# Graph attention's f column goes through DRAM to all partitions, in a four-layer graph kernel ordered by a planner

## The chip, the cores and the metric

The kernel runs on one core of a Trainium2 chip. The metric is the device time of one execution in microseconds (us). The core's engines each work through their own queue of instructions in order: TensorE (PE in the profile, its weight loads PEld), VectorE (DVE), ScalarE (ACT), GpSimd (POOL) and SyncE (SP, which here issues the transfers). They wait for each other through semaphores.

## What is computed

There are 64 graphs of 256 nodes with 256 features each, and an integer adjacency matrix of 256 x 256 for each graph. Four layers follow each other, every one wrapped as `x = layernorm(x + layer(x, adj))`:

```
layer 0: transformer block: 8-head attention masked by adj | adj.T | eye, then a 256-1024-256 feed-forward
layer 1: graph attention (GAT) with bias
layer 2: graph attention, then elu
layer 3: two relational convolutions (root weight, relation adj == 1, divided by the degree), each with elu
```

The change is in the two graph-attention layers. Cut to what matters, one of them is

```
Wh = h @ W                                   # 256 nodes x 256
f, g = Wh @ a1, Wh @ a2                      # one number a node, twice
e = leaky_relu(f[:, None] + g[None, :], 0.2)
e = where(adj > 0, e, -1e9)
out = softmax(e, axis=-1) @ Wh
```

The kernel holds e transposed: the partition is the node that g belongs to, and along the free dimension run the nodes of f. So every partition needs the whole row of 256 f values.

## The kernel before

A graph is two blocks of 128 nodes (NB = 2), and all of a graph's work is float32 apart from masks. Nothing is written out engine by engine by hand. The function `graph(g)` describes one graph's operations one after the other: each has an engine, a planned duration in us (the first number of `pe(...)`, `dve(...)`, `act(...)`, `pool(...)`), the tiles it reads and writes, and for VectorE and GpSimd whether it is taken to use the port that the two share (`"uses"`, `"waits"`). All 64 graphs' operations go into one `Plan`. `Plan.schedule` (line 112) then plays them through as a list scheduler: an operation is ready when its predecessors are done, an engine that is free takes the ready operation with the earliest due time (counted back from `PERIOD`, 46 us a graph), provided that the rings have buffers for its tiles. The order that comes out is the order of issue on every engine. So planned durations do nothing on the chip by themselves; they decide the order, and through it which graph's work stands beside which.

Four details of the planner matter for the change. `LAG` is the time that passes between an operation's end and the moment at which another engine sees it (3.5 for SP, 0.08 to 0.21 for the others). `SWITCH` is added to a matrix operation whose mode (`full`, `row`, `col`: how the array is partitioned) differs from the one before it. A buffer ring ("h" has 3 buffers, "e" 4, "bank" the 8 PSUM banks) bounds how many such tiles are in flight. And the readiness of a follower is

```
seen = end + self.LAG[e]
a.ready = max(a.ready, end if a.engine == e else seen + self.TO.get(a.engine, 0.0))
```

so a follower on the same engine counts as ready at the end, without the lag.

Graph attention is `gat` (line 767). It transposes x (L596, copied to a tile T on L599), multiplies by W widened with the two columns a1 and a2 (L605; `gw`), which leaves Wh, f and g side by side in a PSUM bank, and copies that to the SBUF tile `h` (by VectorE on L778 in layer 1, by ScalarE on L776 in layer 2). `spread` (L785 to L790) then brings f to all partitions: for each block of nodes, the f column, repeated 128 times, is transposed by TensorE against the identity, so that a bank `pf` holds f along its free dimension in every partition. VectorE forms e from it, one instruction for each block (L792: add g, take the minimum with the mask `gm`) and one for the leaky relu (L795); ScalarE takes the exponential (L797); TensorE multiplies e by h (L605 again, "bank<-h,e"); L802 is the reciprocal of the row sum. On GpSimd, L781 squares f and g for a check of the value range, and L619 to L622 compute the reciprocal root of each layer norm, which ScalarE applies on L626.

SyncE's queue holds the loads (adj twice a graph, x, and x again as xr: L579) and the stores of the result (L902).

After the planned part, a few values collected on the way decide whether a general path, lines 930 on, computes everything again in a safer way. It is not taken with these inputs.

Of the kernel before, what the change touches and what calls it, by code (L numbers as in the profile page):

```python
# [17 lines left out]
P = 128  # L18
# [6 lines left out]
RINGS = {"x": 3, "adj": 4, "bits": 2, "am": 2, "gm": 6, "T": 5, "qk": 2, "v": 2, "p": 12, "both": 4, "inv": 1, "ctxT": 2, "X": 9,  # L25
         "xr": 2, "hid": 1, "h": 3, "e": 4, "n": 2, "rel": 3, "hi": 2, "lo": 2, "o": 4}
SMALL = {"mv": 8, "st": 4, "rstd": 8, "r": 6, "rdeg": 4}
# [23 lines left out]
class Plan:  # L51
# [7 lines left out]
    TO = {"PE": 0.06, "POOL": 0.05}  # L59
    SWITCH = 0.2  # L60
    PERIOD = 46.0
# [144 lines left out]
def tile_gnn_stack(ctx: ExitStack, tc: tile.TileContext, t: dict, out: bass.AP):  # L206
# [113 lines left out]
    nc.vector.tensor_copy(ident_b, ident)  # L320
    ones_b = filled([P, P], BF16, "ones_b", 1.0)
    ones = filled([P, HD], F32, "ones", 1.0)
    neghalf = filled([P, NT], F32, "neghalf", -0.5)
    eye = filled([P, N // P, N], BF16, "eye", 0.0)
    for h in range(N // P):
        nc.vector.tensor_copy(eye[:, h, h * P : (h + 1) * P], ident_b)
    gcol, bcol = cols("ln1_g", KB), cols("ln1_b", KB)
# [152 lines left out]
    def main_path(plan):  # L480
# [9 lines left out]
        for name, bufs in SMALL.items():  # L490
            ring(name, bufs)
        plan.ring("bank", 8, bank)

        c_wqkv, c_wo, c_w1, c_w2, c_b1, c_bo = (plan.fixed(w) for w in (wqkv, wo, w1, w2, b1, bo))
# [60 lines left out]
        def graph(g):  # L555
# [9 lines left out]
            def act(cost, issue, reads, writes):  # L565
                op("ACT", cost, issue, reads, writes)

            def pool(cost, issue, reads, writes, port="uses"):
                op("POOL", cost, issue, reads, writes, port=port)

            def new(ring, shape, dtype=F32):
                return plan.tile(ring, shape, dtype)
# [16 lines left out]
            def transposed(xt):  # L589

                xT, pt = new("T", [P, KB, N]), new("bank", [P, KB, N])

                def issue():
                    for kb in range(KB):
                        for i in range(NB):
                            nc.tensor.transpose(pt()[:, kb, i * P : (i + 1) * P], xt()[:, i, kb * P : (kb + 1) * P], ident)  # L596

                pe("full", 0.44, issue, [xt], [pt], [xT])
                act(0.48, lambda: nc.scalar.copy(xT(), pt()), [pt], [xT])  # L599
                return xT  # L600
# [6 lines left out]
            def layer_norm(y):  # L607

                mv, stat = new("mv", [P, NB, 2]), new("st", [P, NB, 6])
                rstd = new("rstd", [P, 2, NB])  # L610

                def stats():
                    for i in range(NB):
                        nc.vector.bn_stats(stat()[:, i, :], y()[:, i, :])  # L614
                    for i in range(NB):
                        nc.vector.bn_aggr(mv()[:, i, :], stat()[:, i, :])  # L616

                def root():
# [10 lines left out]
                dve(1.0, stats, [y], [mv, stat])  # L629
                pool(1.5, root, [mv], [rstd], port="waits")  # L630
                act(1.0, apply, [y, rstd], [y])
# [25 lines left out]
            def projections(xT):  # L657
# [22 lines left out]
                act(0.49, lambda: nc.scalar.copy(v(), pv()), [pv], [v])  # L680
                return qk, v

            def attention(xT, am):
# [6 lines left out]
                for kt in range(NB):  # L690
# [10 lines left out]

                    pe("row", 1.08, scores, [qk], s, [p[kt, r] for r in range(4)])
                    for r in range(4):
                        pr, k = p[kt, r], 8 * g + 4 * kt + r
                        act(0.61, lambda pr=pr, k=k, sr=s[r]: nc.scalar.activation(  # L705
                            pr(), sr(), AF.Exp, accum_out=seen_sum[:, k : k + 1]), [s[r]], [pr])
                        dve(0.60, lambda pr=pr, kt=kt: nc.vector.tensor_tensor(  # L707
                            pr(), pr(), am()[:, kt, None, :].to_broadcast([P, KB, N]), op=ALU.mult), [pr, am], [pr], "uses")
# [5 lines left out]
                for hg in range(KB):  # L714
                    pc = new("bank", [P, 2, N])

                    def values(hg=hg, pc=pc):
# [8 lines left out]

                    pe("col", 1.31, values, [v] + both + list(p.values()), [pc], [ctxT, inv])
                    dve(1.67, lambda hg=hg, pc=pc: nc.vector.reciprocal(inv()[:, hg, :], pc()[:, 1, :]), [pc], [(inv, hg)])  # L728
                    dve(0.34, lambda hg=hg, pc=pc: nc.vector.tensor_tensor(
                        ctxT()[:, hg, :], pc()[:, 0, :], inv()[:, hg, :], op=ALU.mult), [pc, (inv, hg)], [(ctxT, hg)])  # L730
                act(0.61, lambda: nc.scalar.activation(inv(), inv(), AF.Identity, accum_out=seen_inv[:, g : g + 1]), [inv], [inv])
                return ctxT

            def product_plus(lhs, reads, rhs, n, add):

                y, po = tok("X"), new("bank", [P, NB, D])
                for i in range(NB):
                    pe("full", 0.43 * n, lambda i=i: product(po()[:, i, :], lambda c: lhs(c)[:, i * P : (i + 1) * P], rhs, n),
                       reads, [po], [y])
                dve(0.66, lambda: nc.vector.tensor_tensor(y(), po(), add(), op=ALU.add), [po, add], [y])  # L740
                return y
# [25 lines left out]
            def gat(xt, layer, gm, seen, bias, finish):  # L767
# [3 lines left out]
                for i in range(NB):  # L771
# [3 lines left out]
                    if bias is None:  # L775
                        act(0.29, lambda i=i, ph=ph: nc.scalar.copy(h()[:, i, 0 : D + 2], ph()), [ph], [(h, i)])  # L776
                    else:
# [4 lines left out]
                                                          h()[:, :, F_COL : G_COL + 1], op=ALU.mult), [(h, 0), (h, 1)], [], "waits")  # L782
                pf = new("bank", [P, N])

                def spread():  # L785
                    for i in range(NB):
                        nc.tensor.transpose(pf()[:, i * P : (i + 1) * P],
                                            h()[:, i, F_COL : F_COL + 1].to_broadcast([P, P]), ident)

                pe("full", 0.22, spread, [(h, 0), (h, 1)], [pf], [e])  # L790
                for i in range(NB):
                    dve(0.40, lambda i=i: nc.vector.scalar_tensor_tensor(e()[:, i, :], pf(), h()[:, i, G_COL : G_COL + 1],  # L792
                                                                         gm()[:, i, :], op0=ALU.add, op1=ALU.min),
                        [pf, (h, i), gm], [(e, i)])
                dve(0.60, lambda: nc.vector.scalar_tensor_tensor(e(), e(), SLOPE, e(), op0=ALU.mult, op1=ALU.max), [e], [e],  # L795
                    "uses")
                act(0.52, lambda: nc.scalar.activation(e(), e(), AF.Exp), [e], [e])  # L797
                for i in range(NB):
                    po, r = new("bank", [P, HW]), new("r", [P, 1])
                    pe("full", 0.87, lambda i=i, po=po: product(po(), lambda kt: e()[:, kt, i * P : (i + 1) * P],  # L800
                                                                lambda kt: h()[:, kt, :], NB), [e, h], [po], [z, r])
                    dve(0.12, lambda po=po, r=r: nc.vector.reciprocal(r(), po()[:, ONE : ONE + 1]), [po], [r])  # L802
                    finish(i, z, po, r)
# [12 lines left out]
            def layer2(xt, gm):  # L816
                def finish(i, z, po, r):
# [4 lines left out]
                                                                     op1=ALU.add), [po, r, xt], [(z, i)])  # L822
                    dve(0.37, lambda: nc.vector.scalar_tensor_tensor(n(), n(), 1.0, xt()[:, i, :], op0=ALU.min,
                                                                     op1=ALU.add), [n, xt], [n], "uses")
                    dve(0.37, lambda: nc.vector.scalar_tensor_tensor(zi(), n(), -1.0, zi(), op0=ALU.add, op1=ALU.max),
                        [n, (z, i)], [(z, i)], "uses")
# [15 lines left out]
            def conv(h, layer, rel, rdeg):  # L842
# [18 lines left out]
                for j in range(NB):  # L861
# [7 lines left out]

                    pe("full", 0.46, gather, [rel, hi, lo], [pa])  # L870
                    if layer == 0:
# [37 lines left out]

    with tc.tile_pool(name="work", bufs=1) as pools["work"], tc.manual_schedule():  # L910
        main_path(Plan())
# [181 lines left out]
    wrong = nc.values_load(bad_i, min_val=0, max_val=4 * P)  # L1093
    with tc.tile_pool(name="general", bufs=1) as pools["work"], tc.If(wrong > 0):
        w_rel0 = []
        for i in (1, 2):
# [62 lines left out]
```

## Time and profile before

| | us |
|---|---|
| median of 3 runs | 3038.87 |
| lowest, highest of the 3 | 3038.41, 3041.54 |
| the profiled execution | 3041.5 |
| its span, from the first to the last instruction | 3039.6 |
| VectorE busy | 2560.6 (84%) |
| ScalarE busy | 1574.8 (52%) |
| GpSimd busy | 761.8 (25%) |

The profiled execution is 1.9 us longer than its span, and its granted TensorE clock was 0.994. "Busy" counts from an instruction's start to its end, and neighbours overlap in an engine's pipeline, so a mean duration is longer than the time by which one instruction pushes back the next. For that the profile's chain of work is of use: it cuts each stretch of time to the instruction that carried it.

### The profile page before, as it was taken

How to read it: one execution, taken by the hardware profiler on the slowest of the kernel's cores; microseconds unless marked ns; L12 is line 12 of the kernel's file. 1: busy time of each engine (PE TensorE's matmuls, PEld its weight loads, DVE VectorE, ACT ScalarE, POOL GpSimd, SP SyncE). 2: the span in 40 equal slices, each digit the busy share in tenths (PEclk: the TensorE clock that was granted, in tenths of full speed). 3: DMA queues.
4: the chain of work that ended last, by engine and by line, in shares of the span. 5: the costliest groups of instructions: out<-in, count | busy, mean ns of one | idle time of the engine just before them, and what ended most of it. 6: DMA issues, size and time to landing. Idle time of an engine off the chain costs nothing.

```text
span 3039.6 us, 49429 instructions
## 1 busy us (share of the span) xinstructions
PE 2949.0 (97%) x17462; PEld 2257.9 (74%) x17462; DVE 2560.6 (84%) x6368; ACT 1574.8 (52%) x3777; POOL 761.8 (25%) x1877
## 2 busy tenths in 40 slices
PE   8999999999999999999999999999999999999897
PEld 6777767777777777777777777777777777777584
DVE  6889798888797987988889888979889879897857
ACT  3455445555554554555455455545555545555444
POOL 2222222222222222222232222222222223222121
PEclk9999999999999999999999999999999999999999
DMA  5001011111010010010110101100101110001000
GB/s 155 25 22 36 19 34 32 29 28 32 22 32 29 29 36 28 25 32 28 29 32 25 36 22 32 32 29 28 30 27 29 29 31 29 28 25 29 8 11 15
DMA packets 91947, 93.56 MB, mean 31 GB/s; under 512 B 5648, under 2 KB 90896, under 8 KB 91696
## 3 DMA queue, kind: packets, MB, share of 16 engines
q1 hardware_dynamic: 91072, 89.15, 9.9%
q8 instruction: 141, 2.31, 0.3%
q0 software_dynamic: 624, 1.19, 0.2%
q14 instruction: 110, 0.90, 0.1%
HBM read 73.54 MB, written 16.78 MB: 30 GB/s over the span
## 4 chain that ended last, share of the span: by engine, by line
PE 71%; DVE 19%; ACT 4%; POOL 3%; issue 2%; SPq 1%; DMA 0%; POOLq 0%; ACTq 0%; DVEq 0%
PE bank L605 57%; PE bank L596 4%; PE bank L724 3%; PE bank L867 3%; DVE p L707 2%; PE bank L699 2%; PE bank L719 2%; DVE st L614 2%; ACT X L626 1%; POOL rstd L620 1%; ACT p L705 1%; DVE o L877 1%; DVE inv L728 1%; DVE both L711 1%; DVE X L740 1%
## 5 line engine op out<-in xcount | busy, mean ns | idle before, releaser
L619 POOL TENSOR_SCALAR rstd<-mv 128x2 f32<-128x2 f32 x384 | 134.0, 349 | 1535.2 <-DVE mv L616 1388.5
L605 PE MATMUL bank<-T,w 128*128 128x256 f32 x2048 | 480.7, 381 | 2.0 <-ACT T L599 1.4
L605 PE MATMUL bank<-cw,T 128*128 128x512 f32 x1024 | 469.7, 601 | 11.3 <-ACT T L599 8.8
L626 ACT ACTIVATE X<-X,rstd 128x256 f32<-128x256 f32 x640 | 349.8, 596 | 236.8 <-POOL rstd L622 151.2
L605 PE MATMUL bank<-w,hid 128*128 128x256 f32 x2048 | 463.3, 380 | 0.0
L605 PEld LDWEIGHTS bank<-w,hid 128*128 128x128 f32 x2048 | 383.5, 190 | 58.6 <-issue 5.1
L605 PEld LDWEIGHTS bank<-T,w 128*128 128x128 f32 x2048 | 376.6, 190 | 58.2 <-issue 5.1
L707 DVE TENSOR_TENSOR p<-p,am 128x512 f32<-128x512 f32 x512 | 329.0, 683 | 31.6 <-ACT p L705 30.2
L605 PEld LDWEIGHTS bank<-cw,T 128*128 128x128 f32 x1024 | 192.0, 192 | 212.6 <-issue 186.2
L705 ACT ACTIVATE p<-bank 128x512 f32<-128x512 f32 x512 | 300.7, 599 | 46.7 <-PE bank L699 45.9
L620 POOL TENSOR_TENSOR rstd<-rstd,neghalf 128x2 f32<-128x2 f32 x384 | 311.2, 810 | 32.0
L599 ACT COPY T<-bank 128x512 f32<-128x512 f32 x384 | 222.0, 586 | 184.8 <-PE bank L596 181.2
L605 PE MATMUL bank<-h,e 128*128 128x259 f32 x1024 | 251.3, 386 | 9.5 <-ACT e L797 7.1
L605 PE MATMUL bank<-T,wqkv 128*128 128x256 f32 x1024 | 247.4, 384 | 6.6 <-ACT T L599 6.6
L757 ACT ACTIVATE hid<-bank,col_b 128x256 f32<-128x256 f32 x512 | 212.1, 472 | 74.8 <-PE bank L605 72.7
L605 PE MATMUL bank<-gw,T 128*128 128x258 f32 x1024 | 247.1, 382 | 1.3 <-ACT T L599 1.2
L614 DVE BATCH_NORM_STATS2 st<-X 128x6 f32<-128x256 f32 x640 | 239.2, 416 | 5.1
L605 PEld LDWEIGHTS bank<-h,e 128*128 128x128 f32 x1024 | 190.7, 190 | 67.4 <-issue 28.0
L728 DVE RECIPROCAL inv<-bank 128x256 f32<-128x256 f32 x128 | 215.3, 1721 | 8.7 <-PE bank L724 8.7
L605 PEld LDWEIGHTS bank<-T,wqkv 128*128 128x128 f32 x1024 | 188.8, 191 | 37.4 <-ACT T L599 9.8
L605 PEld LDWEIGHTS bank<-gw,T 128*128 128x128 f32 x1024 | 190.0, 190 | 32.1 <-ACT T L599 3.2
L781 POOL TENSOR_TENSOR seen_fg<-h 128x4 f32<-128x4 f32 x128 | 54.8, 428 | 624.0 <-DVE h L778 322.7
(124 smaller groups left out, 4966.6 us busy)
## 6 DMA issues: line engine op xcount, KB each, us to landing
adj<-in_adj_dram SPq DMA_DIRECT2D x128, 256.0 KB, 2.8
x<-in_x_dram SPq DMA_DIRECT2D x64, 256.0 KB, 2.8
xr<-in_x_dram SPq DMA_DIRECT2D x64, 256.0 KB, 2.8
out_dram<-o SPq DMA_DIRECT2D x64, 256.0 KB, 2.1
w<-in_W1T_dram SPq DMA_DIRECT2D x1, 1024.0 KB, 12.2
w<-in_W2T_dram SPq DMA_DIRECT2D x1, 1024.0 KB, 19.0
wqkv<-in_WqkvT_dram SPq DMA_DIRECT2D x1, 768.0 KB, 4.7
cw<-in_w_root_dram SPq DMA_DIRECT2D x2, 256.0 KB, 5.5
```

Source lines behind the costliest of these rows:

```text
L596: nc.tensor.transpose(pt()[:, kb, i * P : (i + 1) * P], xt()[:, i, kb * P : (kb + 1) * P], ident)
L599: act(0.48, lambda: nc.scalar.copy(xT(), pt()), [pt], [xT])
L605: nc.tensor.matmul(dst, lhsT=lhs(c), rhs=rhs(c), start=(c == 0), stop=(c == n - 1))
L614: nc.vector.bn_stats(stat()[:, i, :], y()[:, i, :])
L619: nc.gpsimd.tensor_scalar(rstd()[:, 0, :], mv()[:, :, 1], 1.0, EPS, op0=ALU.mult, op1=ALU.add)
L620: nc.gpsimd.tensor_tensor(rstd()[:, 0, :], rstd()[:, 0, :], neghalf[:, 0:NB], op=ALU.pow)
L626: nc.scalar.activation(y()[:, i, :], y()[:, i, :], AF.Identity, bias=rstd()[:, 1, i : i + 1], scale=rstd()[:, 0, i : i + 1])
L705: act(0.61, lambda pr=pr, k=k, sr=s[r]: nc.scalar.activation(pr(), sr(), AF.Exp, accum_out=seen_sum[:, k : k + 1]), [s[r]], [pr])
L707: dve(0.60, lambda pr=pr, kt=kt: nc.vector.tensor_tensor(pr(), pr(), am()[:, kt, None, :].to_broadcast([P, KB, N]), op=ALU.mult), [pr, am] ...
L724: nc.tensor.matmul(pc()[32 * r : 32 * r + 32, 0, :], lhsT=v()[:, kt, HD * h : HD * (h + 1)], rhs=p[kt, r]()[:, hg, :], start=(kt == 0), st ...
L728: dve(1.67, lambda hg=hg, pc=pc: nc.vector.reciprocal(inv()[:, hg, :], pc()[:, 1, :]), [pc], [(inv, hg)])
L757: act(0.36, lambda f=f, k=k, ph=ph: nc.scalar.activation(hid()[:, f + k, :], ph()[:, k, :], AF.Relu, bias=b1[:, f + k : f + k + 1]), [ph, ...
```

## The change

`spread` goes. In its place SyncE issues two transfers for each graph-attention layer: the first takes the f column out of `h`, one number a partition and block, to a row of 256 numbers in DRAM (a new ring `f_row` of 3); the second reads that row into all 128 partitions of a new SBUF tile `f` (ring of 3). The two instructions that form e read that SBUF tile instead of the bank, and are now planned as using the shared port. Several planned durations are set anew, `SWITCH` goes from 0.2 to 0.1, and two constants of the general path (`ones_b`, `eye`) are built in that path alone. `PERIOD`, `LAG`, the other rings and every other instruction stay.

```diff
-         "xr": 2, "hid": 1, "h": 3, "e": 4, "n": 2, "rel": 3, "hi": 2, "lo": 2, "o": 4}
+         "xr": 2, "hid": 1, "h": 3, "e": 4, "n": 2, "rel": 3, "hi": 2, "lo": 2, "o": 4, "f": 3}
+DRAM = {"f_row": 3}
-    SWITCH = 0.2
+    SWITCH = 0.1
...
-                pf = new("bank", [P, N])
-
-                def spread():
-                    for i in range(NB):
-                        nc.tensor.transpose(pf()[:, i * P : (i + 1) * P],
-                                            h()[:, i, F_COL : F_COL + 1].to_broadcast([P, P]), ident)
-
-                pe("full", 0.22, spread, [(h, 0), (h, 1)], [pf], [e])
+
+                row, pf = new("f_row", [1, N]), new("f", [P, N])
+
+                def column_out():
+                    with nc.allow_non_contiguous_dma(reason="a column"):
+                        nc.sync.dma_start(row().rearrange("o (i p) -> p (o i)", p=P), h()[:, :, F_COL])
+
+                sp(0.45, column_out, [(h, 0), (h, 1)], [row])
+                sp(0.45, lambda: nc.sync.dma_start(pf(), row().to_broadcast([P, N])), [row], [pf])
                 for i in range(NB):
-                    dve(0.40, lambda i=i: nc.vector.scalar_tensor_tensor(e()[:, i, :], pf(), h()[:, i, G_COL : G_COL + 1],
+                    dve(0.35, lambda i=i: nc.vector.scalar_tensor_tensor(e()[:, i, :], pf(), h()[:, i, G_COL : G_COL + 1],
                                                                          gm()[:, i, :], op0=ALU.add, op1=ALU.min),
-                        [pf, (h, i), gm], [(e, i)])
+                        [pf, (h, i), gm], [(e, i)], "uses")
...
```

The planned durations that are set anew, old to new: layer-norm statistics 1.0 to 0.88; scores 1.08 to 0.97; exponential of the scores 0.61 to 0.58; attention values 1.31 to 1.32; reciprocal of the row sums 1.67 to 1.62 and the product with it 0.34 to 0.28; residual add after a product 0.66 to 0.61; the copies of T 0.48, of v 0.49 and of h 0.29 all to 0.47, 0.47 and 0.27; row sum's reciprocal in graph attention 0.12 to 0.08; the two elu steps of layer 2 0.37 to 0.33; the convolution's gather 0.46 to 0.48.

More of the change, by code (lines that the diff above doesn't have):

```diff
@@ L320, in tile_gnn_stack @@
     nc.vector.tensor_copy(ident_b, ident)
-    ones_b = filled([P, P], BF16, "ones_b", 1.0)
     ones = filled([P, HD], F32, "ones", 1.0)
     neghalf = filled([P, NT], F32, "neghalf", -0.5)
-    eye = filled([P, N // P, N], BF16, "eye", 0.0)
-    for h in range(N // P):
-        nc.vector.tensor_copy(eye[:, h, h * P : (h + 1) * P], ident_b)
     gcol, bcol = cols("ln1_g", KB), cols("ln1_b", KB)
@@ L492, in main_path @@
         plan.ring("bank", 8, bank)
+        for name, bufs in DRAM.items():
+            plan.ring(name, bufs, lambda shape, dtype, i, name=name: pools["dram"].tile(shape, dtype, tag=f"{name}{i}", name=name))
         c_wqkv, c_wo, c_w1, c_w2, c_b1, c_bo = (plan.fixed(w) for w in (wqkv, wo, w1, w2, b1, bo))
@@ L569, in pool, with sp @@
                 op("POOL", cost, issue, reads, writes, port=port)
+            def sp(cost, issue, reads, writes):
+                op("SP", cost, issue, reads, writes)
             def new(ring, shape, dtype=F32):
@@ L598, in transposed @@
                 pe("full", 0.44, issue, [xt], [pt], [xT])
-                act(0.48, lambda: nc.scalar.copy(xT(), pt()), [pt], [xT])
+                act(0.47, lambda: nc.scalar.copy(xT(), pt()), [pt], [xT])
                 return xT
@@ L627, in apply @@
                                              scale=rstd()[:, 0, i : i + 1])
-                dve(1.0, stats, [y], [mv, stat])
+                dve(0.88, stats, [y], [mv, stat])
                 pool(1.5, root, [mv], [rstd], port="waits")
@@ L679, in projections @@
                        [pv], [v])
-                act(0.49, lambda: nc.scalar.copy(v(), pv()), [pv], [v])
+                act(0.47, lambda: nc.scalar.copy(v(), pv()), [pv], [v])
                 return qk, v
@@ L700, in scores @@
                                                  rhs=qk()[f, hg, :], start=True, stop=True)
-                    pe("row", 1.08, scores, [qk], s, [p[kt, r] for r in range(4)])
+                    pe("row", 0.97, scores, [qk], s, [p[kt, r] for r in range(4)])
                     for r in range(4):
                         pr, k = p[kt, r], 8 * g + 4 * kt + r
-                        act(0.61, lambda pr=pr, k=k, sr=s[r]: nc.scalar.activation(
+                        act(0.58, lambda pr=pr, k=k, sr=s[r]: nc.scalar.activation(
                             pr(), sr(), AF.Exp, accum_out=seen_sum[:, k : k + 1]), [s[r]], [pr])
@@ L725, in values @@
                                                  rhs=p[kt, r]()[:, hg, :], start=(kt == 0), stop=(kt == NB - 1))
-                    pe("col", 1.31, values, [v] + both + list(p.values()), [pc], [ctxT, inv])
-                    dve(1.67, lambda hg=hg, pc=pc: nc.vector.reciprocal(inv()[:, hg, :], pc()[:, 1, :]), [pc], [(inv, hg)])
-                    dve(0.34, lambda hg=hg, pc=pc: nc.vector.tensor_tensor(
+                    pe("col", 1.32, values, [v] + both + list(p.values()), [pc], [ctxT, inv])
+                    dve(1.62, lambda hg=hg, pc=pc: nc.vector.reciprocal(inv()[:, hg, :], pc()[:, 1, :]), [pc], [(inv, hg)])
+                    dve(0.28, lambda hg=hg, pc=pc: nc.vector.tensor_tensor(
                         ctxT()[:, hg, :], pc()[:, 0, :], inv()[:, hg, :], op=ALU.mult), [pc, (inv, hg)], [(ctxT, hg)])
-                act(0.61, lambda: nc.scalar.activation(inv(), inv(), AF.Identity, accum_out=seen_inv[:, g : g + 1]), [inv], [inv])
+                act(0.62, lambda: nc.scalar.activation(inv(), inv(), AF.Identity, accum_out=seen_inv[:, g : g + 1]), [inv], [inv])
                 return ctxT
@@ L739, in product_plus @@
                        reads, [po], [y])
-                dve(0.66, lambda: nc.vector.tensor_tensor(y(), po(), add(), op=ALU.add), [po, add], [y])
+                dve(0.61, lambda: nc.vector.tensor_tensor(y(), po(), add(), op=ALU.add), [po, add], [y])
                 return y
@@ L775, in gat @@
                     if bias is None:
-                        act(0.29, lambda i=i, ph=ph: nc.scalar.copy(h()[:, i, 0 : D + 2], ph()), [ph], [(h, i)])
+                        act(0.27, lambda i=i, ph=ph: nc.scalar.copy(h()[:, i, 0 : D + 2], ph()), [ph], [(h, i)])
                     else:
@@ L801, in gat @@
                                                                 lambda kt: h()[:, kt, :], NB), [e, h], [po], [z, r])
-                    dve(0.12, lambda po=po, r=r: nc.vector.reciprocal(r(), po()[:, ONE : ONE + 1]), [po], [r])
+                    dve(0.08, lambda po=po, r=r: nc.vector.reciprocal(r(), po()[:, ONE : ONE + 1]), [po], [r])
                     finish(i, z, po, r)
@@ L822, in finish @@
                                                                      op1=ALU.add), [po, r, xt], [(z, i)])
-                    dve(0.37, lambda: nc.vector.scalar_tensor_tensor(n(), n(), 1.0, xt()[:, i, :], op0=ALU.min,
+                    dve(0.33, lambda: nc.vector.scalar_tensor_tensor(n(), n(), 1.0, xt()[:, i, :], op0=ALU.min,
                                                                      op1=ALU.add), [n, xt], [n], "uses")
-                    dve(0.37, lambda: nc.vector.scalar_tensor_tensor(zi(), n(), -1.0, zi(), op0=ALU.add, op1=ALU.max),
+                    dve(0.33, lambda: nc.vector.scalar_tensor_tensor(zi(), n(), -1.0, zi(), op0=ALU.add, op1=ALU.max),
                         [n, (z, i)], [(z, i)], "uses")
@@ L868, in gather @@
                                              start=(c == 0), stop=(c == len(terms) - 1))
-                    pe("full", 0.46, gather, [rel, hi, lo], [pa])
+                    pe("full", 0.48, gather, [rel, hi, lo], [pa])
                     if layer == 0:
@@ L908, in main_path @@
             o.issue()
-    with tc.tile_pool(name="work", bufs=1) as pools["work"], tc.manual_schedule():
+    with (tc.tile_pool(name="work", bufs=1) as pools["work"],
+          tc.tile_pool(name="dram", bufs=1, space=bass.MemoryType.DRAM) as pools["dram"], tc.manual_schedule()):
         main_path(Plan())
@@ L1094, in tile_gnn_stack @@
     with tc.tile_pool(name="general", bufs=1) as pools["work"], tc.If(wrong > 0):
+        ones_b = gen.sb([P, P], BF16, "ones_b")
+        nc.vector.memset(ones_b, 1.0)
+        eye = gen.sb([P, N // P, N], BF16, "eye")
+        nc.vector.memset(eye, 0.0)
+        for h in range(N // P):
+            nc.vector.tensor_copy(eye[:, h, h * P : (h + 1) * P], ident_b)
         w_rel0 = []
```

## The prediction

> **What bounds the kernel now.** I read the busy shares first, then the stages, then the chain of work, then who waits for whom, and last single groups and the transfers.
>
> ```profile
> PE 2949.0 (97%) x17462; PEld 2257.9 (74%) x17462; DVE 2560.6 (84%) x6368; ACT 1574.8 (52%) x3777; POOL 761.8 (25%) x1877
> ```
>
> ```profile
> 0.00:100.00 100.00, 85.44 (x592) 69.95 (x593) 69.02 (x154) 40.00 (x103) 20.38 (x45) 0.95 0.41 121
> 100.00:2800.00 2700.00, 2658.83 (x15786) 2040.90 (x15785) 2316.94 (x5754) 1429.23 (x3436) 697.80 (x1691) 1.00 0.10 29
> 2800.00:3040.00 240.00, 204.73 (x1088) 147.07 (x1086) 174.62 (x463) 105.57 (x239) 43.59 (x141) 0.95 0.04 11
> ```
>
> The second fence gives three stages (busy time of PE, PEld, DVE, ACT, POOL, then granted clock, DMA share, GB/s). From 100 to 2800 us TensorE is busy 98.5% and lacks 41 us; in the last 240 us, where no new graph fills up, it lacks 35 us. VectorE is second with 86% in the middle.
>
> ```profile
> PE 71%; DVE 19%; ACT 4%; POOL 3%; issue 2%; SPq 1%; DMA 0%; POOLq 0%; ACTq 0%; DVEq 0%
> ```
>
> ```profile
> 1516.34 0.59 PE bank L596 x4
> 1516.92 0.22 PE bank L787 x2
> 1517.14 6.91 PE bank L605 x24
> ```
>
> The chain is TensorE for 71%, but VectorE for 19%: TensorE sets the pace, and a late VectorE result often decides. The three pieces (start, us, instructions) show what a `spread` costs where TensorE carries the chain: 0.22 us for its two transposes, not the 273 ns that each is listed with, because they overlap their neighbours.
>
> **What is removed.** Each of 64 graphs has two such pairs: 128 x 0.22 = 28.2 us of TensorE's time. Read in stretches of 40 us, the chain carries 84 of those pairs, 19.7 us. The planner makes a new order around the shorter work, and in the middle stage, with 117 of the 128 pairs (234 of the 256 instructions), TensorE has hardly a gap to lose it in; 117 x 0.22 = 25.7. I take 25 off, with 20 and 28 as ends. With the pairs goes a wait, and one PSUM bank an attention becomes free:
>
> ```profile
> DVE e L792 <- PE bank L787: 29.2, 25, 5.0
> ```
>
> Columns: total us, times, longest. That is VectorE waiting for the transposes in 25 of 128 cases; the transfer takes this wait's place, so I count no gain for it.
>
> **The two instructions that form e** now read f from SBUF instead of PSUM. The nearest rows are L821, the same instruction with one input in PSUM, and L823, with all in SBUF:
>
> ```profile
> 1495.34 0.88 DVE X L821 x2
> 1496.21 0.67 DVE n L823 x2
> ```
>
> 0.44 against 0.335 each, so 256 x 0.105 = 27 us less VectorE time. In the chain's stretches L792 carried 68 instructions and 27.1 us; at 0.335 they would take 22.8. I take 4 us off; ends 0 (VectorE then waits for something else) and 7 (68 x 0.105).
>
> Two SBUF inputs also take the port shared with GpSimd. The row: the reciprocal root's multiply on L621 has a median of 196 ns and a longest of 754, and its mean is 313, so GpSimd already is held up beside such work. The new use is 4 x 0.335 = 1.3 us in some 47 us a graph; four GpSimd instructions each for 384 norms, held up 3% oftener by 0.2 us or so, make under 10 us of GpSimd's time, and GpSimd carries 3% of the chain: under 0.5 us, counted as nothing. [...]
>
> **What is added: two transfers in series, on SyncE.** Issue costs nothing on the path by itself: SP's longest idle waits are 43.9 and 93.4 us, and 256 more issues at 0.37 are 95 us of 3040. What counts is the latency from h to f.
>
> ```profile
> adj<-in_adj_dram SPq DMA_DIRECT2D x128, 256.0 KB, 2.8
> ...
> out_dram<-o SPq DMA_DIRECT2D x64, 256.0 KB, 2.1
> ...
> col_ln_g<-in_ln_g_dram POOLq DMA_DIRECT2D x1, 1.0 KB, 7.8
> ```
>
> The last column is us from issue to landing. *The column's way out* is 256 pieces of 4 bytes; the trace has no such store. A store of 256 pieces of 1 KB, the result, lands after 2.1 us. Its pieces took 46 ns each and sixteen follow each other on one of 16 DMA engines, 0.74 us, so without any movement 1.4 would be left: the lower end. The upper end is the only column of single numbers in the trace, a load at the start beside the weights and through GpSimd's queue: 7.8. I take 2.1, because queue, direction and piece count are those of the store. *The row's way in* is 128 pieces of 1 KB, half of an adj load: 2.8 less half of 0.74, so 2.4; ends 2.0 and 2.8. Together 4.5 us, ends 3.4 and 10.6; two semaphore steps between queues may add 0.2.
>
> [...]
>
> What did the plan allow? Planned, the column takes 0.45 of SP, the row follows at once (same engine, no lag), takes 0.45 and is seen 3.5 later: 4.4 us. The order in which the changed program's instructions stand, weighed with the chain's times (0.43 for a 256-wide float32 product, 0.11 a transpose), has 4 to 5 us of TensorE work between the column's issue and e's first instruction in 69 of 128 cases, a median of 4.4. So the plan puts VectorE's e just where f is planned to land, and a later landing is met by a VectorE that waits, with the next layer norms and masks queued behind. Actual 4.5 to 4.7 against 4.4: up to 0.3 us late. In the chain's stretches 34 of 128 attentions had e on the chain, so 34 x 0.15 is 5 us added. Below nothing is excluded: the order is fixed, and f landing early moves no instruction. At the upper end, 10.6, it is 6.2 x 34 = 211 us.
>
> Behind the row's wait on SP stand a load in 79 of 128 cases, a store or another column in nearly all others. A load delayed by 2 us is covered, since in before VectorE waited for loads only 6.7 us (xr) and 0.8 (adj) in all. A column that stands behind another attention's row (26 cases, 8 of them at once) starts up to 2 us late: some 8 x 2 us, a quarter on the chain, 4 us, which I leave inside the range.
>
> **The end.** In the last 23 us of TensorE work before the final convolutions, eight attentions stand close, with 3.9 to 5.6 us of TensorE work between the last product into h and the first with e; the path is now about 0.4 (copy) + 4.6 + 1.4 (e) + 0.6 (exponential), 7 us. In before it needed some 3, with 2.8 to 11.4 of work. The last graph has two attentions in series, each longer by about 4 us; other graphs' work covers part. I add 6; ends 0 and 10.
>
> **Planned durations.** They cost nothing themselves and change the order everywhere. The new ones lie nearer to the chain's pieces (0.67 for two of L823 against 0.33 planned each). What a better order could win is bounded by the 41 us that TensorE lacks in the middle, and I see no reason that a worse one loses more: from -41 to +41, taken as 0.
>
> **The sum.** -25 - 4 + 5 + 6 = -18 us against the profiled execution's 3041.5 (span 3039.6 and 1.9 around it). That execution is 2.6 above the median of three, so on the median's scale 3038.9 - 18 = 3021.
>
> **Rivals.**
> *Late column (slower).* The 4-byte writes land later than the 1 KB ones and the wait at L787 becomes a longer one at the transfer. For: the only column in the trace took 7.8, and the plan has no slack behind 4.4. Against: that one was at the start. It decides from 23/34 = 0.7 us late on average (18 + 5 = 23 to make up), that is 5.1 us for both. At a column of 3.3 both take 5.7 + 0.2, so 1.5 late: 34 x 1.5 = 51, and the time is 3021 - 5 + 51 = 3067.
> *A better order as well (faster still).* Shorter plan, one bank free, 1% less VectorE: if two thirds of the 41 us goes too, 3021 - 27 = 2994.
> *It does nothing for the pace.* If VectorE's 19% and the end decide, TensorE only waits where it used to transpose: what stays is -4 + 5 and the worse end, so about 3039.
>
> **How the numbers follow.** The forecast, 3021 (its own range 3006 to 3033), has 0.50; late column 0.24; better order 0.14; no effect 0.12. About 0.2%, 6 us, is what a measurement of this kernel can tell from no change. Faster by more: 0.48 + 0.14 + 0.01 = 0.63; slower by more: 0.22 + 0.04 = 0.26; the rest 0.11. The range from 2990 to 3062 leaves out the better half of one rival and the worse half of another, some 0.18.
>
> **What would show it.** Right: TensorE's busy time down by about 50 us as listed (256 x 273 ns overlaps; its own 28 on the chain), the column landing at about 2.1 and the row at 2.4, e's instructions near 415 ns instead of 473, and VectorE's wait for f under 30 us in all. Wrong: a column landing above 2.8, VectorE waiting for f by more than 100 us, TensorE waiting for ACT's exponential (7.1 us in before) by several tens, or a middle stage below 98% busy.

## The result, and the profile after

The changed kernel takes 4213.45 us (median of four runs, 4212.58 to 4216.83) against 3040.2 for the kernel before beside it: a ratio of 1.3862, 95% interval 1.3838 to 1.3886. I had forecast 3021, in a range from 2990 to 3062. The profiled execution took 4213.6 with a span of 4211.9.

The page's first part, and the two lines of its fourth:

```profile
PE 3215.4 (76%) x17206; PEld 2424.9 (58%) x17206; DVE 2573.7 (61%) x6364; ACT 1577.7 (37%) x3777; POOL 703.4 (17%) x1877
...
PE 43%; DMA 31%; DVE 15%; issue 7%; ACT 3%; POOL 1%; SPq 0%; DVEq 0%; ACTq 0%; POOLq 0%
PE bank L607 35%; DMA f_row<-h 21%; DMA f<-f_row 10%; PE bank L598 2%; PE bank L870 2%; DVE e L795 2%; DVE p L709 2%; PE bank L701 1%; DVE e L798 1%; PE bank L726 1%; DVE inv L730 1%; DVE st L616 1%; DVE o L880 1%; PE bank L721 1%; ACT X L628 1%
```

The 256 transposes are gone (17462 to 17206 instructions), and yet TensorE is busy 266 us longer and idle for 996.5 us instead of 90.6; 266.4 + 905.9 is the whole difference of the spans, 1172.3. Transfers, 0% of the chain before, carry 31% of it. The transfers and the wait for them (issues: us to landing last; waits: total, times, longest):

```profile
f<-f_row SPq DMA_DIRECT2D x128, 128.0 KB, 5.0
...
f_row<-h SPq DMA_DIRECT2D x128, 1.0 KB, 8.4
```

```profile
DVE e L795 <- DMA f<-f_row: 1116.3, 128, 13.7
```

8.4 + 5.0 = 13.4 us from the column's issue to f, where the plan has 4.4: 9.0 us late, in every one of 128 attentions, and 1173 / 128 is 9.2. One of them in the timeline, where a row is start, us, engine, line:

```profile
2022.01 0.37 SPq L790 DMA_DIRECT2D f_row<-h  x1
...
2026.13 3.60 PE L607 MATMUL bank<-cw,T 128*128 128x512 f32 x8
...
2030.58 0.34 SPq L793 DMA_DIRECT2D f<-f_row  x1
2035.55 0.88 DVE L795 SCALAR_TENSOR_TENSOR e<-f,h,gm 128x256 f32<-128x256 f32 x2 [8.64 <-DMA f<-f_row]
...
2037.92 3.37 PE L607 MATMUL bank<-h,e 128*128 128x259 f32 x8 [8.20 <-issue]
```

VectorE stands for 8.64 us at the head of its queue; TensorE has work until 2029.73 (2026.13 + 3.60), then runs dry for 8.2. The same stretch cut up (busy time of PE, PEld, DVE, ACT, POOL, then granted clock, DMA share, GB/s):

```profile
2022.80:2023.20 0.40, 0.40 (x6) 0.38 (x4) 0.40 (x2) 0.40 (x2) 0.00 (x0) 1.00 0.37 3
2023.20:2030.40 7.20, 6.52 (x24) 3.73 (x22) 3.68 (x6) 1.59 (x4) 0.00 (x0) 1.00 0.00 0
2030.40:2033.20 2.80, 0.00 (x0) 0.00 (x0) 0.00 (x0) 0.00 (x0) 0.00 (x0) 1.00 0.00 0
2033.20:2035.20 2.00, 0.00 (x0) 0.00 (x0) 0.00 (x0) 0.00 (x0) 0.00 (x0) 0.68 0.24 66
2035.20:2036.00 0.80, 0.00 (x0) 0.00 (x0) 0.45 (x2) 0.00 (x0) 0.00 (x0) 0.50 0.00 0
```

And the fall of the clock in finer steps:

```profile
2033.60:2034.00 0.40, 0.00 (x0) 0.00 (x0) 0.00 (x0) 0.00 (x0) 0.00 (x0) 0.89 0.42 95
2034.00:2034.40 0.40, 0.00 (x0) 0.00 (x0) 0.00 (x0) 0.00 (x0) 0.00 (x0) 0.50 0.21 46
```

Two things are to be seen. The column's packets are over at 2023.2, and then for 7.2 us the trace has no DMA packet at all: the column is not slow to send, and the time passes behind its last packet. And between 2033.60, where it is still 1.00, and 2034.00, that is 3.9 to 4.3 us after TensorE ran dry, its granted clock falls to 0.50. It is still 0.50 in the stretch up to 2040.40, 2.5 us after TensorE has begun again, and 1.00 from 2040.80. So the next products crawl: eight in 3.37 us, where before, in the first row here, they took 1.91. The group of them (before, then after; busy us, mean ns of one) grew by 200 of the 266 us:

```profile
1522.14 1.91 PE L605 MATMUL bank<-h,e 128*128 128x259 f32 x8
...
L605 PE MATMUL bank<-h,e 128*128 128x259 f32 x1024 | 251.3, 386 | 9.5 <-ACT e L797 7.1
...
L607 PE MATMUL bank<-h,e 128*128 128x259 f32 x1024 | 451.3, 615 | 775.6 <-ACT e L800 397.5
```

That is one case, followed in the trace; over the whole execution the granted clock was 0.871, against 0.994 before. The clock was nowhere in my sum.

### The profile page after: what moved, and what is told of

Read it like the earlier page. It is cut to its first block, busy times and chain, and to the rows that moved or that the text cites. A ratio compares the mean times of both kernels' runs of the same rounds, so it can differ in the third digit from the quotient of the medians.

```text
span 4211.9 us, 49579 instructions
## 1 busy us (share of the span) xinstructions
PE 3215.4 (76%) x17206; PEld 2424.9 (58%) x17206; DVE 2573.7 (61%) x6364; ACT 1577.7 (37%) x3777; POOL 703.4 (17%) x1877
## 4 chain that ended last, share of the span: by engine, by line
PE 43%; DMA 31%; DVE 15%; issue 7%; ACT 3%; POOL 1%; SPq 0%; DVEq 0%; ACTq 0%; POOLq 0%
PE bank L607 35%; DMA f_row<-h 21%; DMA f<-f_row 10%; PE bank L598 2%; PE bank L870 2%; DVE e L795 2%; DVE p L709 2%; PE bank L701 1%; DVE e L798 1%; PE bank L726 1%; DVE inv L730 1%; DVE st L616 1%; DVE o L880 1%; PE bank L721 1%; ACT X L628 1%
## 5 line engine op out<-in xcount | busy, mean ns | idle before, releaser
L607 PE MATMUL bank<-h,e 128*128 128x259 f32 x1024 | 451.3, 615 | 775.6 <-ACT e L800 397.5
L607 PEld LDWEIGHTS bank<-h,e 128*128 128x128 f32 x1024 | 309.0, 316 | 899.2 <-issue 794.9
L795 DVE SCALAR_TENSOR_TENSOR e<-f,h,gm 128x256 f32<-128x256 f32 x256 | 113.3, 481 | 1116.3 <-DMA f<-f_row 1116.3
L621 POOL TENSOR_SCALAR rstd<-mv 128x2 f32<-128x2 f32 x384 | 116.8, 304 | 2882.7 <-DVE mv L618 2550.5
L800 ACT ACTIVATE e<-e 128x512 f32<-128x512 f32 x128 | 80.6, 629 | 1158.8 <-DVE e L798 1136.2
L607 PEld LDWEIGHTS bank<-T,w 128*128 128x128 f32 x2048 | 392.9, 196 | 69.9 <-issue 10.8
L607 PEld LDWEIGHTS bank<-w,hid 128*128 128x128 f32 x2048 | 390.3, 193 | 59.5 <-issue 5.8
L607 PE MATMUL bank<-T,wqkv 128*128 128x256 f32 x1024 | 259.0, 397 | 6.0 <-ACT T L601 5.6
```

The costliest lines, as they stand in the source:

```text
L607: nc.tensor.matmul(dst, lhsT=lhs(c), rhs=rhs(c), start=(c == 0), stop=(c == n - 1))
L795: dve(0.35, lambda i=i: nc.vector.scalar_tensor_tensor(e()[:, i, :], pf(), h()[:, i, G_COL : G_COL + 1], gm()[:, i, :], op0=ALU.add, op1=A ...
```

## Experiments

Two theories. *Latency*: f lands 9 us after the place where the order needs it. *Order*: the new planned durations made a bad order. Times are medians, ratios against the kernel before on the same chip.

**1. The durations without the transfers, and the transfers without the durations.**

The first version (e1) has the new durations and `SWITCH`, but f goes through `spread` as before and the instructions that form e keep 0.40 and read the bank. The second (e2) has the two `sp(...)` operations and e at 0.35 with `"uses"`; all other durations and `SWITCH` are as before.

> The new planned durations and SWITCH 0.1 alone; f still goes through TensorE's transposes, and the instructions that form e keep their 0.40 and read the bank. If the transfers' latency is what costs the 1173 us, this lies within 1% of before: 3010 to 3070, VectorE waits for the transposes some 30 us, and TensorE is busy 96% or more. If the order that the new durations make is what costs, it is above 3500.

> The two transfers alone, with before's planned durations and SWITCH 0.2. Latency theory: 4150 to 4270, like the whole change, with the column landing near 8.4 us, the row near 5.0, and VectorE waiting for f about 1100 us. If the order is at fault: near 3050.

Measured: durations alone 3045.98 (1.0017, 1.0007 to 1.0026). Transfers alone 4085.3 (1.3431, 1.3404 to 1.3457), with landings of 7.9 and 4.7 us and a wait for f of 988.8. The transfers are the cause: without them the durations and their order cost some 6 us. That expectation's time, 4150 to 4270, was missed all the same: the two landings make 12.6 us here, not 13.4, and the time is 128 us below the change's.

**2. The planner is told how long the transfers take.** A follower of a transfer, on SyncE too, counts as ready after a lag of the transfer's own, and due times are set back by it.

```diff
-                seen = end + self.LAG[e]
+                seen = end + (self.LAG[e] if o.lag is None else o.lag)
...
-                    a.ready = max(a.ready, end if a.engine == e else seen + self.TO.get(a.engine, 0.0))
+                    a.ready = max(a.ready, end if a.engine == e and o.lag is None else seen + self.TO.get(a.engine, 0.0))
...
-                sp(0.45, column_out, [(h, 0), (h, 1)], [row])
+                sp(0.45, column_out, [(h, 0), (h, 1)], [row], 8.1)
```

(The row's transfer gets 4.8.)

> The whole change, but the planner is told that the row can start 8.1 us after the column's issue is over, and that f is seen 4.8 us after the row's, so that it puts other work between. Latency theory: the transfers land as late as after the change (8.4 and 5.0) but VectorE's wait for f falls from 1116 to under 150 us, the granted clock is back at 0.98 or more, and the time is 3000 to 3100. Rival: the 13 us cannot be hidden, because the rings (h 3, e 4) hold too few attentions or SyncE's queue is blocked while the row waits for the column; then the wait stays above 500 us and the time above 3400.

Measured: 3072.13 (1.0100, 1.0083 to 1.0116), landings of 8.5 and 4.0. The first part of its page:

```profile
PE 2944.8 (96%) x17206; PEld 2242.3 (73%) x17206; DVE 2562.2 (83%) x6364; ACT 1578.9 (51%) x3777; POOL 705.4 (23%) x1877
```

And from its waits (total, times, longest):

```profile
DVE e L795 <- DMA f<-f_row: 59.5, 31, 5.2
```

The transfers are as slow as ever; the wait for f is 59.5 us in 31 cases, the granted clock is 0.989, and 1141 of the 1173 us are gone. The rival, that the rings or SyncE's queue would not let so much be hidden, fell. So the cost was not the transfers as such but their place in the order. The kernel is still 1% slower than before.

**3. What the removal is worth at best.** A constant tile stands for f, so that its distribution is left out: once with the new durations, once with before's.

Against the change (`neg_row` is that tile; the second version does the same to the kernel before):

```diff
-                row, pf = new("f_row", [1, N]), new("f", [P, N])
...
-                sp(0.45, column_out, [(h, 0), (h, 1)], [row])
-                sp(0.45, lambda: nc.sync.dma_start(pf(), row().to_broadcast([P, N])), [row], [pf])
+                pf = plan.fixed(neg_row)
```

> Neither transposes nor transfers: a constant tile in SBUF stands for f, so the distribution of f is left out. It prices what the removal could have brought at best with the new durations: by the prediction's sum, 25 (TensorE) and 4 (VectorE) less than the durations alone, whose time was 3046, so 3017 (3005 to 3030). If TensorE does not set the pace: 3040 to 3046.

> Before's planned durations and SWITCH 0.2, neither transposes nor transfers: a constant tile in SBUF stands for f, so its distribution is left out. It prices the removal without the new order. By the prediction's sum (25 and 4 us): 3012 (3005 to 3022). If the removal is worth what it was with the new durations (3034 against 3046): 3025 to 3031.

Measured: 3034.21 (0.9978, 0.9968 to 0.9987) with the new durations, 3026.93 (0.9951, 0.9934 to 0.9967) with the old. Against its own partner each is better by 12 and 14 us. That is half of the 29 I had counted, so both expectations by my sum missed; the other figure given for the old durations, 3025 to 3031, held. On the new durations TensorE's busy time did fall by 25.5 us (2963.4 to 2937.9), but its idle time grew by 11.1. This also bounds the idea: with these two sets of durations, f at no cost wins 12 to 14 us. And between experiments 2 and 3 lie 38 us (3072 against 3034), though f's wait is mostly hidden. Whether they come from the 59.5 us of it that are left, from each graph's longer chain or from loads held up on SyncE was not separated. In the middle stage TensorE is busy 2623.1 of 2700 us with it, 2650.6 without; the row of this stage, first of the version that is told its lags (experiment 2):

```profile
100.00:2800.00 2700.00, 2623.13 (x15429) 1999.39 (x15428) 2294.18 (x5699) 1422.47 (x3415) 631.02 (x1673) 1.00 0.14 34
```

And of the version without f, on the new durations:

```profile
100.00:2800.00 2700.00, 2650.56 (x15554) 2020.22 (x15553) 2321.43 (x5754) 1425.27 (x3440) 679.38 (x1692) 1.00 0.10 29
```

**4. Where the 13.4 us come from: the first probe.** On the order of e1, each attention issues one more transfer that nobody waits for.

```diff
                 pe("full", 0.22, spread, [(h, 0), (h, 1)], [pf], [e])
+                kind = seen % 7
...
```

(`kind` chooses which of the seven this attention issues.)

> The order of the new durations with TensorE's transposes, plus one transfer for each attention that nobody waits for, of seven kinds in turn (18 or 19 of each), to read their time from issue to landing. 1: the f column, 256 pieces of 4 B to a DRAM row with a stride, as in the change; 2: 256 pieces of 64 B to DRAM; 3: 256 pieces of 512 B to DRAM; 4: the f column to a DRAM row in the order in which the pieces are read, without a stride; 5: the f column to a row in one partition of SBUF; 6: one DRAM row of 1 KB, written long ago, to all 128 partitions; 7: 128 different DRAM rows of 1 KB. If the 4-byte write to DRAM is what is slow: 8 us for the first and the fourth, 2 to 3 for the third and the fifth, the second between. If a DMA of single numbers is slow whatever it writes: the fifth is also 8. If reading one row by all is slow: the sixth 5 and the seventh 2.4; if the row was slow only because it had just been written: the sixth 2.4 too. Time within 2% of the kernel with the durations alone.

Medians from issue to landing: the f column to DRAM as in the change 8.5 us; pieces of 64 B 1.9; of 512 B 2.1; the column in the order of reading 7.3; the column to a row in SBUF 2.4; one old DRAM row to all partitions 3.4; 128 different rows 2.6. From the probe's DMA issues (times, KB each, us to landing last):

```profile
d<-h SPq DMA_DIRECT2D x18, 128.0 KB, 2.1
f<-in_bo_dram SPq DMA_DIRECT2D x18, 128.0 KB, 3.4
f<-in_x_dram SPq DMA_DIRECT2D x18, 128.0 KB, 2.6
...
d<-h SPq DMA_DIRECT2D x19, 16.0 KB, 1.9
one<-h SPq DMA_DIRECT2D x18, 1.0 KB, 2.4
```

So neither a small piece (64 B is as fast as 512) nor single numbers as such (2.4 to SBUF) are slow: 256 pieces of 4 B into one KB of DRAM are. The row is slow in two steps: 0.8 us where all partitions read the same KB, and 0.6 to 1.6 more in the kernels (4.0 to 5.0), where it has just been written. Whether the fresh write is the reason for this second step was not tested.

**5. What makes the column slow: the second probe, the same bytes in another order, and a third probe.**

> Like the first probe: the order of the durations alone, one transfer an attention that nobody waits for, six kinds in turn, from SBUF to DRAM. 1: 16 pieces of 4 B; 2: 256 pieces of 8 B, each in a slot of 32 B; 3: 256 pieces of 32 B; 4: 256 pieces of 4 B, each in a slot of 64 B; 5: 256 pieces of 4 B, each in a slot of 512 B; 6: 256 pieces of 64 B. If each small write costs a read and a write of its own, one after the other on each DMA engine (16 pieces an engine), the first takes 2.5 or less and the second, fourth and fifth stay at 8. If pieces that share a stretch of DRAM wait for each other, the fourth or the fifth falls to 2 to 3 while the first stays above 3. The sixth is 1.9 again; the third tells where between 4 and 64 B the cost ends.

Measured: 16 pieces 1.3 us; 8 B in slots of 32 B 2.4; 32 B dense 1.8; **4 B in slots of 64 B 2.2, in slots of 512 B 1.9**; 64 B 1.9. "A read and a write each" falls, since 4 B in slots of their own are fast. Pieces that share a stretch of DRAM are nearer, but that theory had the 16 pieces, which share 64 B, above 3 us. I took the stretch to be 64 B and an engine's own pieces to wait for each other, and tested that in the change itself: the pieces of 8 neighbouring partitions and both blocks, which I assumed to share a DMA engine (no trace shows which engine carries which piece), go to 16 stretches of 64 B instead of one or two.

```diff
-                        nc.sync.dma_start(row().rearrange("o (i p) -> p (o i)", p=P), h()[:, :, F_COL])
+                        nc.sync.dma_start(row().rearrange("o (b i k) -> k b (o i)", b=8, i=NB), h()[:, :, F_COL])
...
```

The instruction that forms e reads the row in the new order; it takes a mean of 642 ns instead of 481.

> [...] Same bytes, same number of 4-byte pieces, same plan. If an engine's small writes to one 64-byte stretch wait for each other (the second probe: 2.2 us with a slot of 64 B each, against 8.5 dense), the column lands at 2.0 to 2.6, the row at 3.4 to 5.0, VectorE's wait for f falls from 1116 us to 100 to 400, and the time is 3090 to 3400. If dense 4-byte writes are slow whatever their order: still 4200.

Measured: 3953.77 (1.3002, 1.2981 to 1.3024), the column at 7.4 and the row at 4.0. With that assumption the theory fell: the same dense KB in another order is nearly as slow.

The third probe has six kinds, in the order of its forecasts: 128 pieces of 8 B and 64 of 16 B, dense (1 KB each); 256 of 4 B in slots of 8, 16 and 32 B (2, 4 and 8 KB); and 17 of 4 B, dense, which I assumed to go by one DMA engine.

> As in the second probe, six kinds of transfer from SBUF to DRAM in turn that nobody waits for. [...] Theory of the shared stretch: small writes into the same KB or so are served one after the other whoever sends them, (8.4 - 1.9) us / 256 = 25 ns each; then 5.1, 3.5, 5.1, 3.5, 2.7 and under 2 us. Theory of the engine: a DMA engine's own small writes close to each other wait, some 0.4 us each with 16 an engine; then 5, 3.5, 8, 7 or less, 2.4 and 8.

The third probe's DMA issues:

```profile
da<-h SPq DMA_DIRECT2D x22, 1.0 KB, 3.2
db<-h SPq DMA_DIRECT2D x22, 1.0 KB, 1.8
dc<-h SPq DMA_DIRECT2D x21, 1.0 KB, 3.7
dd<-h SPq DMA_DIRECT2D x21, 1.0 KB, 2.9
de<-h SPq DMA_DIRECT2D x21, 1.0 KB, 2.2
```

These are the first five kinds in their order. The sixth kind shows no landing in the trace, so whether one engine or all matter stays open. What is shown: with 256 pieces the landing falls from 8.5 over 3.7, 2.9 and 2.2 to 1.9 as they are spread over 1, 2, 4, 8 and 128 KB. So in these rows the number of pieces in each KB decides, together with how many there are: the 16 packed into 64 B took 1.3. 25 ns a piece for each KB is not its law: it forecast 5.1, 3.5, 5.1, 3.5 and 2.7, every one too high. Nor is the theory of the engine right, with 5, 3.5, up to 8, up to 7 and 2.4. Why the pieces in one stretch slow each other was not found.

**6. The row in SBUF.** This takes the slow write away and keeps two transfers.

```diff
-                row, pf = new("f_row", [1, N]), new("f", [P, N])
+                row, pf = new("f_one", [1, N]), new("f", [P, N])
...
-                sp(0.45, lambda: nc.sync.dma_start(pf(), row().to_broadcast([P, N])), [row], [pf])
+                sp(0.45, lambda: nc.sync.dma_start(pf(), row()[:, None, :].to_broadcast([1, P, N])), [row], [pf])
```

(`f_one` is an SBUF ring of 1, f a ring of 2. The row holds the two blocks interleaved, and the instruction that forms e reads it so.)

> The whole change, but the column goes to a row in one partition of SBUF instead of DRAM, and the second transfer reads that partition 128 times (rings: 2 buffers for f, 1 for the row, because SBUF is full; the row holds the two blocks interleaved and the instruction that forms e reads it so). The planner still assumes 4.4 us. If the 4-byte writes to DRAM are the cause, the column lands at 2.4, the row at 2.4 to 3.4, VectorE's wait for f falls from 1116 us to 50 to 150, the granted clock is above 0.98, and the time is 3020 to 3120. If any chain of two transfers breaks this order, it stays above 3500.

> The same with the planner told of 2.2 us after the column's issue and 2.6 after the row's. The latency is then planned for: 3010 to 3060. If what makes the version with DRAM and its lag told 1% slower than before is the longer chain of each graph, this one, with 8 us less of it an attention, lies below 3050; if it is the transfers' presence as such, it stays at 3070.

Measured: 3564.21 (1.1717, 1.1698 to 1.1737) and, with lags told, 3364.0 (1.1062, 1.1044 to 1.1081). The DMA issues of the first:

```profile
f<-f_one SPq DMA_DIRECT2D x128, 128.0 KB, 6.3
...
f_one<-h SPq DMA_DIRECT2D x128, 1.0 KB, 2.4
```

The column lands at 2.4 as expected, but one partition read 128 times takes 6.3. So the times missed, and so did the lag that I told (2.6 for a row that needs over twice that). The first lies above 3500, where the rival had it, that any two transfers break this order; but what is slow here is the row, not the pair as such. Yet this gives the price of a microsecond. With the change's durations and a planner that assumes 4.4, the sum of the landings and the time go together: 8.7 us and 3564, 11.4 and 3954, 13.4 and 4213: 144 and 130 us for each us. That is about 128 attentions, each paying in full. It is rough: the middle version carries 41 us more of VectorE's work (256 times 642 against 481 ns).

**7. The told planner with before's durations.**

> The transfers with the planner told of 8.1 and 4.8 us, with before's planned durations and SWITCH 0.2. If the new durations cost some 6 us wherever they are used (3046 against 3040, 3034 against 3027), this is 3066 against 3072. If with the long transfers the durations matter more, it differs by over 15 us in either direction.

Measured: 3254.2 (1.0699, 1.0675 to 1.0723), 182 us above experiment 2, not 6 below. The wait for f is as well hidden (77.1 us), but another is not. From TensorE's waits:

```profile
PE bank L598 <- DMA x<-in_x_dram: 87.1, 16, 9.5
```

And from those of SyncE's queue:

```profile
SPq L792 <- DMA f_row<-h: 612.6, 121, 10.0
```

Here SyncE's queue stands still while a row waits for its column, 612.6 us in all. In experiment 2 it stood as long (599.8), so this is not the difference. The load of a graph's x is: it comes too late 16 times, once at the start as before and 15 times later. One of these:

```profile
2042.01 0.36 SPq L789 DMA_DIRECT2D f_row<-h  x1
2042.61 0.37 SPq L581 DMA_DIRECT2D x<-in_x_dram  x1
...
2054.40 1.09 PE L598 MATMUL bank<-ident,x 128*128 128x128 f32 x4 [6.57 <-DMA x<-in_x_dram]
```

The load was issued at once, 0.6 us behind a column, and TensorE could use it 11.8 us later; before, such a load landed after a median of 2.8. In 14 of the 15 cases the load was issued 0.6 to 7.3 us behind a column whose row was not yet issued, and was used 6.5 to 12.4 us after its issue. So a column that has not landed holds up what is issued behind it. The landings of this run are not in its trace, but others show it: in the first probe and the reordered column of experiment 5, all 19 transfers that were issued while a column was in flight, as far as the traces tell, landed 0.8 to 3.9 us after that column, and 4.1 to 11.0 us after their own issue. 34 of the 64 loads of x stand in such a place here, 17 in experiment 2. The planner knows of no such delay, so whether an order runs into it is luck. Of the 182 us, 135 are idle time of TensorE, 81 of them these loads (87.1 against 6.2), and 47 are longer busy time, at a granted clock of 0.964 against 0.989. What the remaining 54 of idle time come from was not separated.

## Why the prediction was wrong

- *TensorE sets the pace, and the removal is worth 25 us.* The sign held, the size did not: 12 to 14 us (experiment 3). The chain's own 19.7 was the nearer row.
- *The instructions that form e get cheaper by 4 us.* Failed: a mean of 481 ns with f in SBUF against 473 from the bank, and two still take 0.88. I had compared L821 with L823, which differ in two things; L823 has a constant, L821 and the e instruction a per-partition scalar from a tile. The bank is not the dearer part, so what is left of the two is the scalar; no run changes it alone.
- *The column lands at 2.1 us because queue, direction and piece count are those of the result's store.* This is the step that failed: 8.4. The one condition that the row did not share, the size and density of the pieces, was the one that counted. The upper end I had, 7.8 from a load of single numbers, was nearly the measured value, though that load went the other way, beside other traffic, so the nearness may be luck.
- *The row lands at 2.4, between 2.0 and 2.8.* Failed: 5.0. An adj load reads different rows, at rest; this reads one KB 128 times, just written (3.4 for such a row at rest).
- *The plan has 4.4 us and no slack; VectorE waits at the head of its queue.* Right, and only the lateness was wrong, 9.0 us instead of 0.15: 125 to 128 of 128 waited for f in the change and in each version with a row in DRAM and no lag told. No run shows the 0.2 us for two semaphore steps: the row was issued a median of 17 ns after the column's landing, and e began 25 ns after the row's (in the 33 and 58 cases whose landing is in the trace of the change).
- *Late f costs 34/128 of its lateness.* This failed too, and it made the rival too cheap: with the true lateness it gives 9.0 x 34 = 306 us, and 9.0 x 128 = 1152 is close to the 1173 that were paid. The share of attentions with e on the chain was measured when e was in time. At 9 us late all 128 pay in full, and the clock falls on top (0.871 against 0.994). My upper end for the latency, 10.6, was priced at 211 us; by experiment 6's slope I estimate some 800. The rival "late column" had the mechanism right, and its point, 0.7 us late, would have told that anything near 7.8 is a disaster.
- *The durations cost 0, within 41.* The durations alone cost 6 us. With the lags told they decided over 182, with the plain transfers over 128, part of which are the later landings (experiment 1).
- *A load delayed behind the row's wait is covered.* Nearly so in the first told order, where VectorE waits 14.2 us for xr (6.7 before) and TensorE for x no longer than before; not in the second (experiment 7). I had counted the wait in the queue, not the slow landing behind a column.

## What to carry to other kernels

Price a transfer by a row that shares its piece size and its density in memory, not only its queue and its count; where none does, take the far end for the decision. In this statically ordered kernel a transfer cost about what it landed later than the order assumed, once for each use (130 to 144 us for each us, with 128 uses), and little up to that point (38 us at most); so tell the planner the landing time, for followers on the same queue too, and see what is issued behind a slow transfer. When a bound engine is made to wait, ask what its clock does (0.50 here after 3.9 to 4.3 us).

## What the runs showed of the hardware

- 256 writes of 4 B into one KB of DRAM land after 7.3 to 8.5 us, into 2 KB after 3.7, into 16 KB after 2.2, while 256 writes of 64 B take 1.9 and the same 4 B into one SBUF partition 2.4. In the one followed above the trace has no DMA packet for 7.2 us of the wait.
- A transfer issued while such a column was in flight landed 0.8 to 3.9 us after the column, in 19 of 19 cases (experiment 7): 4.1 to 11.0 us after its issue, where loads had a median of 2.8 before and the stores 2.1.
- Reading one DRAM row into 128 partitions took 3.4 us against 2.6 for 128 different rows, 4.0 to 5.0 when the row had just been written, and 6.3 from a single SBUF partition.
- TensorE's granted clock fell from 1.00 to 0.50 between 3.9 and 4.3 us after it ran dry, and was back at 1.00 2.5 to 2.9 us after it had begun again (one case).
- Before, GpSimd's multiply on L621 took 194 to 197 ns in the 101 cases in which VectorE ran beside it only instructions with an input in a PSUM bank, and 347 to 635 ns, with a median of 616, in the 23 in which it ran only the product of p and am, both in SBUF. In all, GpSimd was busy 703.4 us in the change, 761.8 before.
